# A selective-scan megakernel: the chunk's y is copied first in ACT's step, stores are issued behind their data, and some readers get more links

## The chip, the cores and the metric

The kernel runs on one core of a Trainium2 chip. The metric is the device time of one execution in microseconds; before the change it is 19824.35 us, the median of three runs (19803.24 to 19829.89).

## The reference

Four images of 64 x 64 positions and 96 channels go through four layers. Each layer is `x = x + mixer(norm(x))` and then `x = x + ffn(norm(x))`; the feed-forward part is two small quantised matrix products. The mixer of layer 0 is a gated linear recurrence. The mixers of layers 1 to 3 are selective scans with 192 inner channels, 16 states and four orders of reading the image (by rows, by columns, and both backwards). Cut to what matters:

```
xz = x @ in_proj_w.T;  xi, z = split(xz)
xc = silu(conv3x3_depthwise(xi))
xs = [xc by rows, xc by columns, both reversed]           # 4 orders, L = 4096 steps
dts, B, C = split(xs @ x_proj);  delta = softplus(dts @ dt_proj + bias)
h_t = exp(delta_t * A) * h_(t-1) + delta_t * u_t * B_t    # per channel, 16 states
y_t = sum over states of h_t * C_t  + D * u_t
y = sum of the four orders, put back in place
x = x + (norm(y) * silu(z)) @ out_proj.T
```

## The kernel before

**Stages, chunks and tiles.** After layer 0 (`gated`) the scans of layers 1 to 3 run in 12 stages, one for each image and layer. A stage has two directions, four segments of 1024 steps and three chunks of 128 rows; each chunk has 16 tiles, one for each state. So a stage has 384 tiles and all stages 4608. A tile's *step* in its chunk, 0 to 15, is `n` in the code; `k` counts tiles through all stages.

**What a tile does.** ACT makes the decay `da` (`decays`, line 898), PE spreads a row of B over 128 partitions into `bc` (`b_rows`, 904), DVE multiplies `bc` by `du` and scans (`scan`, 913), ACT copies the last column (`carry`, 929), POOL multiplies `h` by the `c` rows, which SP loads from DRAM two tiles ahead (`c_rows`, 888; `times_c`, 935), and PE adds the product to the chunk's `acc` three tiles later (`accumulate`, 955). When 16 products are in, ACT copies `acc` to `y` and SP stores it (`store`, 966); that falls in step 3 of the next chunk. Buffers: two of `bc`, three of `da` and of `h`, six of `c`, one of `acc`.

**The order on each engine** is the order in which the Python code calls it; no engine reorders. The loop of `scans` (line 993 on) issues for tile `k`: `carry(k-1)`, loads and decay of `k+2`, `b_rows(k+1)`, `times_c(k-1)`, `store` when due, `scan(k)`, and `accumulate(k-3)`. Between the product and the scan of a tile, `beside` (1018) lets other work issue instructions.

**That other work** is written as Python generators, called chains. Every `yield` ends a *link*: what stands between two yields is issued in one go, and the next link at a later turn. The next chunk's preparation and the next segment's get one link per tile. A `Job` (708) does everything between two stages for another image; it gets `rate` links per tile for each of its chains. `between` (616) is such a job: `first` loads the scans' `y` in both orders (3 MB and the first strip), then per strip of 512 positions run `join_orders` (transposes `y_t`, copy to `yt`, statistics), `mixer_out` (normalise, gate, `out_proj`, sum `x1`) and `feed_forward`, then `take_in` (norm, `in_proj`, `z`) and `convolve`. `gate_z` (557) applies silu to `z` and stores it. If a job is not done by tile 356 of a stage, the rest is issued at once.

**SP's queue** issues all transfers, also in order, and waits in front of a transfer whose data or buffer isn't ready.

All operations are recorded by one helper, so the profile shows line 78 for nearly all; they are told apart by the names of their tiles.

Of the kernel before, what the change touches and what calls it, by code (L numbers as in the profile page):

```python
# [21 lines left out]
NS = 16  # L22
# [3 lines left out]
T = 1024  # L26
MM = 512
# [72 lines left out]
def metaformer(ctx: ExitStack, tc: tile.TileContext, x, l0_ab, l0_rest, ssm, ffn, out):  # L100
# [212 lines left out]
    def join_orders(im, s, hold):  # L313

        yr, yc = hold["in"].pop(s)
        if s + 1 < NSTRIP:
            load_y(im, s + 1, hold)
        cols_a, part_c = hold["cols"]
        yt = sb(2, "yt", [128, G, DI])

        def join(ps, g):

            t0, r0 = 128 * g, SR * s + 2 * g
            o, hi = ps[:, g % 2, 0:128], ps[:, g % 2, 128:DI]
            pe.matmul(o, yr[:, t0 : t0 + 128], ident, start=True, stop=False)
            for r in range(2):
                v = cols_a.rearrange("p (c r) -> p r c", r=HW)[:, r0 + r, :]
                pe.matmul(o[64 * r : 64 * r + 64], v, ident, start=False, stop=True)
            yield
            pe.matmul(hi, yc[:, t0 : t0 + 128], ident[0:64, 0:64], start=True, stop=False)  # L330
            for r in range(2):
                for k in range(2):
                    p = slice(64 * k, 64 * k + 64)
                    v = part_c.rearrange("p (c r) -> p r c", r=HW)[p, r0 + r, :]
                    q = 64 * r + 32 * k
                    pe.matmul(
                        hi[q : q + 32], v, ident[p, p], start=False, stop=True, tile_position=(64 * k, q)
                    )

        for pair in range(2):  # L340
            ps = bank("y_t")[:, 0 : 2 * DI].rearrange("p (g c) -> p g c", g=2)
            yield from join(ps, 2 * pair)
            yield
            yield from join(ps, 2 * pair + 1)
            yield
            act.copy(yt[:, 2 * pair : 2 * pair + 2, :], ps)
            release()
            yield pair == 0
        yield
        norm = Norm()  # L350
        yield from norm.measure(yt, DI, 1e-5)
        hold["y", s] = yt, norm

    def mixer_out(im, layer, s, hold):

        w = weights[layer].w
        yt, norm = hold.pop(("y", s))
        zl, zh, xr = load_z(im, s)
        yield from norm.settle()
        yield  # L360
        normalise(yt, yt, DI, norm.r, norm.nm)
        yield
        yield True
        g = []
        for i, (a, b, z) in enumerate(((0, 128, zl), (128, 192, zh))):
            ps = bank("y_c")
            transpose_strip(ps, yt, a, b)
            yield
            v = sb(1, f"u{i}", [128, MM])
            m = b - a  # L370
            sc, bias = (w[0:m, W_LN + 2 * i + k : W_LN + 2 * i + k + 1] for k in range(2))
            act.activation(v[0:m], ps[0:m], AF.Identity, bias=bias, scale=sc)
            release()
            yield i == 0
            g.append(v)
            if i == 0:
                continue
            for v, z, m in ((g[0], zl, 128), (g[1], zh, 64)):
                pool.tensor_tensor(v[0:m], v[0:m], z[0:m], ALU.mult)
                yield  # L380
        yield True
        ps = bank("out_proj")
        for q in range(G):
            t = slice(128 * q, 128 * q + 128)
            o = ps[:, C * q : C * q + C]
            pe.matmul(o, g[0][:, t], w[:, W_OUT : W_OUT + C], start=True, stop=False)
            pe.matmul(o, g[1][0:64, t], w[0:64, W_OUT + C : W_OUT + 2 * C], start=False, stop=True)
            yield
        yield
        x1 = sb(2, "x1", [128, G, C])  # L390
        dve.tensor_tensor(x1, xr, ps[:, 0 : G * C].rearrange("p (g c) -> p g c", g=G), ALU.add)
        release()
        yield
        norm = Norm()
        yield from norm.measure(x1, C, 1e-5)
        hold["x", s] = x1, norm
# [159 lines left out]

    def gate_z(im, s, hold):
        if s < NSTRIP:
            t = slice(s * MM, (s + 1) * MM)
            for z, a in zip(hold["z"].pop(s), (0, 128)):  # L560
                act.activation(z, z, AF.Silu)
                sp.dma_start(out=im.z[a : a + z.shape[0], t], in_=z)

    def convolve(im, layer, s, hold):

        lo, hi = hold["pads"].pop(s)
        taps = weights[layer]
        w = taps.w
        raw = []
        groups = (  # L570
            [(taps.lo[:, t, :], lo[:, t // 3 : t // 3 + SR, t % 3 : t % 3 + HW]) for t in range(9)],
            [(taps.hi[:, t, :], hi[:, 0:SR, t : t + HW]) for t in range(3)]
            + [(taps.hi[0:64, 3 + t, :], hi[0:64, 2 : 2 + SR, t : t + HW]) for t in range(3)],
        )
        for i, group in enumerate(groups):
            ps = bank("conv")
            for at, (lhs, rhs) in enumerate(group):
                pe.matmul(ps, lhs, rhs, start=at == 0, stop=at == len(group) - 1)
                yield
            v = sb(1, f"u{i}", [128, MM])  # L580
            act.copy(v, ps)
            release()
            yield i == 0
            raw.append(v)
        for i, v in enumerate(raw):
            act.activation(v, v, AF.Silu, bias=w[:, W_CB + i : W_CB + i + 1])
        gate_z(im, s + 1, hold)
        yield
        yield
        t = slice(s * MM, (s + 1) * MM)  # L590
        cols_a, part_c = hold["cols"]
        sp.dma_start(out=im.u[0, 0:64, t], in_=raw[0][0:64])
        sp.dma_start(out=im.u[1, 0:64, t], in_=raw[0][64:128])
        sp.dma_start(out=im.u[2, 0:64, t], in_=raw[1][0:64])
        for p, src, dst, c0, nc_ in (
            (slice(0, 128), raw[0], cols_a, 0, HW),
            (slice(0, 64), raw[1], part_c, 0, HW // 2),
            (slice(64, 128), raw[1], part_c, HW // 2, HW // 2),
        ):
            pool.tensor_copy(  # L600
                dst[p].rearrange("p (c r) -> p r c", r=HW)[:, SR * s : SR * s + SR, :],
                src[p].rearrange("p (r c) -> p r c", c=HW)[:, :, c0 : c0 + nc_],
            )
            if p.start or p.stop == 128:
                yield
        if s == NSTRIP - 1:
            yield
            sp.dma_start(out=im.u[1, 64:128, :], in_=cols_a[0:64])
            sp.dma_start(out=im.u[0, 64:128, :], in_=cols_a[64:128])
            for k in range(2):  # L610
                sp.dma_start(
                    out=im.u[2, 64:128, k * L // 2 : (k + 1) * L // 2],
                    in_=part_c[64 * k : 64 * k + 64],
                )

    def between(im, layer, dst=None):
# [8 lines left out]
        def first():  # L625
            if layer:
# [6 lines left out]
                        in_=im.y[2, 64:128, k * L // 2 : (k + 1) * L // 2],  # L633
                    )
                load_y(im, 0, hold)
            yield
            yield
            yield

        yield [Chain(first())]  # L640
        done = {"y": 0, "x": 0, "end": 0}
# [55 lines left out]
        def convolves():  # L697
            yield lambda: done["in"] > 0
            gate_z(im, 0, hold)
            for s in range(NSTRIP):  # L700
                yield lambda: done["in"] > min(s + 1, NSTRIP - 1)
                yield True
# [60 lines left out]
    def prepare_segment(item, sg):  # L763
# [38 lines left out]
        for k in range(2):  # L802
# [3 lines left out]
            yield from project(ps, m, m + NC2, k)  # L806
            act.copy(sg.rows[0:NC2, cols], ps[0:NC2])
            release()
        sp.dma_start(out=sg.cs, in_=sg.rows[0:NC2])

    def prepare_chunk(item):
# [48 lines left out]
    def scans(stages, jobs, pac):  # L860
# [94 lines left out]
        def accumulate(k):  # L955
# [7 lines left out]
                    add_quarters(i, i.yf, stacked, True, False)  # L963
            add_quarters(i, h, stacked, False, n == NS - 1)

        def store(i):
            y = sb(2, "y", [128, T])
            act.copy(y, i.acc)
            for j in range(2):
                for k in range(2):  # L970
                    o = 64 * (j ^ k)
                    t = i.seg * T + k * MM
                    sp.dma_start(
                        out=i.im.y[i.chunk, 64 * j : 64 * j + 64, t : t + MM],
                        in_=y[o : o + 64, j * MM : (j + 1) * MM],
                    )

        chain = segment = None
# [15 lines left out]
        for k in range(last + 5):  # L994
# [23 lines left out]
            def beside():  # L1018
# [5 lines left out]
                        drain(segment, work)  # L1024
                work()

            if 0 <= k - 1 <= last:
                carry(k - 1)
            if k + 2 <= last:
# [5 lines left out]
                b_rows(k + 1)  # L1035
            if 0 <= k - 1 <= last:
                times_c(k - 1)
            if k >= 4 and (k - 4) % NS == NS - 1:
                store(items[(k - 4) // NS])
            if k <= last:  # L1040
                scan(k, beside)
            if 0 <= k - 3 <= last:
                accumulate(k - 3)
            settle()
# [238 lines left out]
    for at in range(len(stages)):  # L1283
        jobs.append([])
        if at + 1 < len(stages):
            im, layer = stages[at + 1]
            jobs[-1].append(Job(between(im, layer - 1), 1.65))

        for im in {10: images[:2], 11: images[2:3]}.get(at, ()):
            jobs[-1].append(Job(between(im, 3, im.dst), 2.6))  # L1290
    with tc.tile_pool(name="pac", bufs=1, space=bass.MemoryType.PSUM) as pac:
        scans(stages, jobs, pac)
    Job(between(images[-1], 3, images[-1].dst), patience=1).finish()
# [123 lines left out]
```

## Time and profile before

| what | us |
|---|---|
| median of three runs | 19824.35 |
| the profiled execution's own time | 19851.56 |
| its span | 19849.8 |
| layer 0, until the first scan | 1962.6 |
| the scans, first start to last end | 17596.9 |
| a stage of layer 1, 2 or 3 (the first ten) | 1428.6 to 1466.9 |
| the last two stages | 1493.6 and 1575.4 |
| after the last scan | 290.2 |
| DVE busy in all | 17714.5 |
| POOL, PE and ACT busy in all | 15487.4, 16411.2 and 12300.6 |

In the profile `h<-da,carry,bc` is the scan, `bc<-du,bc` the product in front of it, `bc<-bs,sel` the spreading on PE, `c<-h,c` POOL's product and `acc<-c,twice` the sum on PE. Behind a bar stands the idle time of the engine just before a group, with what ended it. A wait "DVE bc <- PE bc" means that DVE stood idle in front of the product until PE had written `bc`. The mean granted TensorE clock is 0.814 of full speed.

### The profile page before, as it was taken

The numbers are of one execution on the slowest core, as the hardware profiler recorded it, in microseconds if no ns is written. First come the engines' busy times: TensorE is split into PE (matmuls) and PEld (weight loads), VectorE is DVE, ScalarE is ACT, GpSimd is POOL, SyncE is SP. The second block draws the span as 40 slices with busy tenths as digits, with TensorE's granted clock in tenths as the row PEclk, the third lists the DMA queues.
The fourth block names the chain that finished last, engine by engine and source line by source line (L and its number), as shares of the span: only waits on it lengthen the run. The fifth ranks groups of instructions, "written<-read, shape, count | busy, mean of one in ns | idle before, by whom it ended". The sixth has DMA issues, their size and how long they took to land. (4 is left out here: it accounts for less than half of the span.)

```text
span 19849.8 us, 224201 instructions
## 1 busy us (share of the span) xinstructions
PE 16411.2 (83%) x70656; PEld 4815.3 (24%) x70656; DVE 17714.5 (89%) x13832; ACT 12300.6 (62%) x19398; POOL 15487.4 (78%) x10086
## 2 busy tenths in 40 slices
PE   8898788787787888888887887887888888888786
PEld 3333121121121222222222222222222222222223
DVE  6656999999999999999999999999999999989884
ACT  3444665665665665665665665666666666666664
POOL 3333888888888888888888888888888888888884
PEclk9899786796787787887797797797797787888886
DMA  0001666666666666666666666666666666666663
GB/s 19 15 22 36 164 179 176 166 182 173 168 185 174 168 180 184 167 183 180 167 182 177 170 183 181 167 183 182 165 188 174 174 185 173 170 188 169 165 176 91
DMA packets 1233005, 3142.45 MB, mean 158 GB/s; under 512 B 428048, under 2 KB 428176, under 8 KB 1225680
## 3 DMA queue, kind: packets, MB, share of 16 engines
q1 hardware_dynamic: 1231824, 3128.11, 59.1%
q8 instruction: 570, 9.34, 0.2%
q14 instruction: 611, 5.01, 0.1%
HBM read 2819.03 MB, written 308.28 MB: 158 GB/s over the span
## 5 line engine op out<-in xcount | busy, mean ns | idle before, releaser
L78 POOL TENSOR_TENSOR c<-h,c 128x1024 f32<-128x1024 f32 (+1 forms) x4992 | 11327.0, 2275 | 3532.4 <-DVE h L78 1479.8
L78 DVE TENSOR_TENSOR_SCAN h<-da,carry,bc 128x1024 f32<-128x1024 f32 x4608 | 10797.2, 2343 | 532.1 <-POOL c L78 17.0
L78 PE MATMUL acc<-c,twice 64*64 64x512 f32 x36864 | 6212.0, 750 | 21.8 <-POOL c L78 21.7
L78 ACT ACTIVATE da<-delta,decay 128x1024 f32<-128x1024 f32 x4608 | 5280.5, 1147 | 1497.1 <-DVE h L78 1474.3
L78 DVE TENSOR_TENSOR bc<-du,bc 128x1024 f32<-128x1024 f32 x4608 | 5567.8, 1208 | 499.7 <-PE bc L78 473.6
L78 PE MATMUL bc<-bs,sel 96*128 96x512 bf16 x9216 | 3392.6, 456 | 2350.8 <-DVE h L78 2239.7
L78 ACT COPY carry<-h 128x1 f32<-128x1 f32 x3456 | 649.7, 188 | 3366.3 <-DVE h L78 3360.1
L78 PEld LDWEIGHTS <-sel 96*128 96x128 bf16 x9216 | 551.3, 101 | 7304.2 <-DVE h L78 5491.0
L78 PEld LDWEIGHTS acc<-c,twice 64*64 64x64 f32 x36864 | 1132.6, 153 | 2805.1 <-issue 1888.6
L78 ACT ACT_TABLE_LOAD x1158 | 1485.7, 1283 | 37.8 <-DVE mv L78 21.5
L78 PE MATMUL conv<-pad,tap_lo 128*128 128x512 f32 x1728 | 904.9, 633 | 0.0
L78 PE MATMUL dt_proj<-rows,w 12*128 12x512 f32 x1152 | 832.1, 809 | 6.1 <-ACT delta L78 6.1
L78 ACT ACTIVATE du<-e,ones 128x1024 f32<-128x1024 f32 x576 | 659.3, 1145 | 200.8 <-POOL delta L78 195.7
L78 ACT ACTIVATE c<-c,l_bias 128x512 f32<-128x512 f32 x384 | 263.4, 686 | 771.8 <-PE c L78 770.4
L78 POOL TENSOR_TENSOR delta<-delta,du 128x1024 f32<-128x1024 f32 x288 | 679.4, 2359 | 71.4 <-ACT du L78 69.3
L78 PE MATMUL x_proj_b<-u,xp 128*108 128x512 f32 x1152 | 694.4, 720 | 42.5 <-DMA xp<-in_ssm 14.5
L78 PE MATMUL x_proj_c<-u,xp 128*32 128x512 f32 x1152 | 632.0, 662 | 76.0 <-ACT rows L78 67.1
L78 POOL TENSOR_TENSOR e<-e,du 128x1024 f32<-128x1024 f32 x288 | 679.1, 2358 | 2.4 <-ACT du L78 2.4
L78 POOL TENSOR_TENSOR du<-delta,u 128x1024 f32<-128x1024 f32 x288 | 679.6, 2360 | 0.1
L78 POOL TENSOR_TENSOR delta<-delta,e 128x1024 f32<-128x1024 f32 x288 | 678.1, 2355 | 0.1
L78 PE MATMUL conv<-pad,tap_hi 128*128 128x512 f32 (+1 forms) x1152 | 597.5, 620 | 0.6 <-ACT u L78 0.4
L78 DVE TENSOR_TENSOR_SCAN h<-da,l_carry,bc 128x512 f32<-128x512 f32 x384 | 491.5, 1280 | 42.1 <-POOL c L78 2.0
(154 smaller groups left out, 15512.1 us busy)
## 6 DMA issues: line engine op xcount, KB each, us to landing
c<-cs SPq DMA_DIRECT2D x9216, 256.0 KB, 4.1
u<-u SPq DMA_DIRECT2D x288, 512.0 KB, 6.6
y<-y SPq DMA_DIRECT2D x1152, 128.0 KB, 3.2
y<-y SPq DMA_DIRECT2D x144, 512.0 KB, 6.9
xr<-x SPq DMA_DIRECT2D x224, 192.0 KB, 5.3
u<-u SPq DMA_DIRECT2D x288, 128.0 KB, 3.5
pad<-y SPq DMA_DIRECT2D x288, 128.0 KB, 4.9
z<-zl SPq DMA_DIRECT2D x96, 256.0 KB, 2.0
```

The source lines that it names most:

```text
L78: ins = f(*a, **k).ins
```

## The change

- `join_orders` and `mixer_out` get one more `yield` each: one ahead of the statistics of `yt`, one ahead of the sum `x1` on DVE.
- `gate_z` applies silu alone; the stores of `z` are in a new `store_z`, two links later.
- `first` waits nine links instead of three after its loads, where the layer is 1 or more.
- `prepare_segment` gets one more `yield` ahead of the store of `cs`.
- `store` is cut in two: `take` copies `acc` to `y` as the first of ACT's instructions in the tile, ahead of `carry`; the transfers of `store` are issued behind `scan` and what `beside` issues.
- The jobs' rates go from 1.65 to 1.72 and from 2.6 to 2.8 (layer 0's job keeps 2.6).

```diff
@@ join_orders
             yield pair == 0
+        yield
         yield
         norm = Norm()
         yield from norm.measure(yt, DI, 1e-5)
@@ mixer_out
             yield
         yield
+        yield
         x1 = sb(2, "x1", [128, G, C])
@@ gate_z
     def gate_z(im, s, hold):
         if s < NSTRIP:
+            for z in hold["z"][s]:
+                act.activation(z, z, AF.Silu)
+
+    def store_z(im, s, hold):
+        if s < NSTRIP:
             t = slice(s * MM, (s + 1) * MM)
             for z, a in zip(hold["z"].pop(s), (0, 128)):
-                act.activation(z, z, AF.Silu)
                 sp.dma_start(out=im.z[a : a + z.shape[0], t], in_=z)
@@ convolve
         gate_z(im, s + 1, hold)
         yield
         yield
+        store_z(im, s + 1, hold)
@@ between, first
-            yield
-            yield
-            yield
+            for _ in range(9 if layer else 3):
+                yield
@@ between, convolves
             gate_z(im, 0, hold)
+            yield
+            yield
+            store_z(im, 0, hold)
@@ prepare_segment
             release()
+        yield
         sp.dma_start(out=sg.cs, in_=sg.rows[0:NC2])
@@ scans
+        def take(i):
+            i.y = sb(2, "y", [128, T])
+            act.copy(i.y, i.acc)
+
         def store(i):
-            y = sb(2, "y", [128, T])
-            act.copy(y, i.acc)
...
-                        in_=y[o : o + 64, j * MM : (j + 1) * MM],
+                        in_=i.y[o : o + 64, j * MM : (j + 1) * MM],
@@ scans, the loop
+            full = items[(k - 4) // NS] if k >= 4 and (k - 4) % NS == NS - 1 else None
+            if full is not None:
+                take(full)
             if 0 <= k - 1 <= last:
                 carry(k - 1)
...
                 times_c(k - 1)
-            if k >= 4 and (k - 4) % NS == NS - 1:
-                store(items[(k - 4) // NS])
             if k <= last:
                 scan(k, beside)
+            if full is not None:
+                store(full)
@@ the jobs
-            jobs[-1].append(Job(between(im, layer - 1), 1.65))
+            jobs[-1].append(Job(between(im, layer - 1), 1.72))
...
-            jobs[-1].append(Job(between(im, 3, im.dst), 2.6))
+            jobs[-1].append(Job(between(im, 3, im.dst), 2.8))
```

## The prediction

> **What bounds the kernel now.** I read the page first, then the waits of DVE, PE and POOL between 1986 and 19560 us (the scans), then the timeline around the longest idle stretches.
>
> ```profile
> span 19849.8 us, 224201 instructions
> ...
> PE 16411.2 (83%) x70656; PEld 4815.3 (24%) x70656; DVE 17714.5 (89%) x13832; ACT 12300.6 (62%) x19398; POOL 15487.4 (78%) x10086
> ...
> L78 DVE TENSOR_TENSOR_SCAN h<-da,carry,bc 128x1024 f32<-128x1024 f32 x4608 | 10797.2, 2343 | 532.1 <-POOL c L78 17.0
> ...
> L78 DVE TENSOR_TENSOR bc<-du,bc 128x1024 f32<-128x1024 f32 x4608 | 5567.8, 1208 | 499.7 <-PE bc L78 473.6
> ```
>
> DVE paces the scans. One tile costs a product of 1.21 us, a scan of 2.34 and about 0.1 between them: the undisturbed tile of the timeline is 3.6 us. The scans run from 1963 to 19560, 17597 us, in which DVE is busy 17115; another 0.5 ms is the short step between product and scan. Idle stretches over 0.3 us add up to only 627 us, 23 of which are the very first tile. So no edit here can win more than about 600 us (3%), and what it wins is a DVE wait that goes.
>
> ```profile
> DVE bc L78 <- PE bc L78: 473.6, 295, 22.2
> DVE rows L78 <- ACT bs L78: 29.6, 15, 3.9
> DVE x L78 <- PE out_proj L78: 29.3, 24, 2.9
> DVE st L78 <- ACT yt L78: 22.0, 22, 2.7
> ```
>
> Those are DVE's waits in the scans: total, count, longest. Nearly all are for `bc`, which PE writes. PE works in order, so a late `bc` means that PE was held in front of it. By step of the chunk (16 tiles), the idle before `bc` is largest in steps 4 and 5 (61 and 86 us), just behind the copy of `y`, then 9 (76), 0 (54, with the first tile's 23) and 6 (44, where the jobs' first loads are read).
>
> ```profile
> PE acc L78 <- ACT y L78: 156.9, 146, 2.9
> ...
> PE y_t L78 <- DMA pad<-y: 94.3, 11, 24.4
> ```
>
> These are two of PE's own waits in the same stretch; both are what the change goes for.
>
> **Part 1: nine links instead of three behind the first loads.** A job reads 3 MB (`cols_a`, `part_c`) and the first strip before its first `y_t`. The trace shows 11 such reads in the scans: eight at a stage's start (DVE idle 4.9 to 6.1 us each, 43.3 in all) and three later (22.2, 14.3 and 11.2), each of these followed by one more wait of 2.57: 99 us. The built orders put the first `y_t` in tile 7 of a stage instead of 4, and 5 tiles behind the late loads instead of 2: three tiles, 10.8 us, more. PE's own wait at a stage's start, 3.8 to 6.8 us, would be gone. But does DVE get all of it?
>
> ```profile
> 6264.07 2.35 POOL L78 TENSOR_TENSOR c<-h,c 128x1024 f32<-128x1024 f32 x1 [1.25 <-DVE h L78]
> ...
> 6272.41 2.35 DVE L78 TENSOR_TENSOR_SCAN h<-da,carry,bc 128x1024 f32<-128x1024 f32 x1
> ...
> 6275.27 0.77 PE L78 MATMUL y_t<-ident,pad 128*128 128x128 f32 x2 [6.62 <-DMA pad<-y]
> ...
> 6277.49 4.71 POOL L78 TENSOR_TENSOR c<-h,c 128x1024 f32<-128x1024 f32 x2 [11.06 <-DMA c<-cs]
> ...
> 6280.63 1.23 DVE L78 TENSOR_TENSOR bc<-du,bc 128x1024 f32<-128x1024 f32 x1 [5.88 <-PE bc L78]
> ...
> 6281.99 2.35 DVE L78 TENSOR_TENSOR_SCAN h<-da,carry,bc 128x1024 f32<-128x1024 f32 x1
> ```
>
> No. POOL is idle for 11.06 us at the same place, and for another reason: its `c` rows were issued behind the 3 MB and landed 17 us later (6259.2 to 6276.3), where the median is 4.1. More links do not move those. `h` has three buffers, so the scan at 6281.99 needs POOL's product of three tiles before, the first of the pair from 6277.49, which ended at 6279.84. Without PE's wait that scan would be due at 6272.41 + 3.6 = 6276.0 and start at about 6279.9: of 5.9 us some 3.9 stay and 2 go. Eight times 2 is 16 us. The same working for the late three (next scans due every 3.6 us, held by the product three tiles before) leaves 14.0 of 24.8, 3.0 of 13.8 and 6.1 of 16.9: 32 us. Together 48; the ends are 25 (what is left is worse) and 99.
>
> The Trainium skill says the same of the queue, and it speaks against this edit: by "DMA: Bandwidth & Descriptors", section "Queues, rings and completion order", each DMA engine takes descriptors in ring order, and all of SP's transfers share one row. By that rule alone the `c` rows must wait for the 3 MB whatever the reader does, which gives the 48; if it did not hold, the 99.
>
> **Part 2: y's copy first in ACT's step.** The copy stood behind `carry` and the decay two tiles ahead, which wait for the scan. `acc` has one buffer, so PE's first matmul of the next chunk waits for the copy, and `bc` waits behind it.
>
> ```profile
> 15909.79 0.61 ACT L78 ACTIVATE zh<-zh 64x512 f32<-64x512 f32 x1
> 15910.31 0.17 ACT L78 COPY carry<-h 128x1 f32<-128x1 f32 x1
> 15910.49 1.28 ACT L78 ACT_TABLE_LOAD   x1
> 15911.78 1.15 ACT L78 ACTIVATE da<-delta,decay 128x1024 f32<-128x1024 f32 x1
> 15912.84 0.99 ACT L78 COPY y<-acc 128x1024 f32<-128x1024 f32 x1
> ```
>
> Here `acc` was complete at 15905.5 and the copy could have started when `zh` ended, 2.4 us sooner; DVE idled 3.35 us before the `bc` behind it. I took all 288 copies so: start minus the later of "`acc` complete" and "ACT free of what stands ahead of `carry`". The mean is 0.8 us, the largest about 3.4. Where a wait for `bc` over 0.3 us follows within four tiles, the smaller of the two is won: 37 places, 43 us, those of part 1 left out. At all 37 POOL's product of three tiles before leaves over 5 us, so it holds nothing. What the copy can now hold up when `acc` is late: `carry` (read 48 tiles later), the decay (1.15 us) and the job's ACT work. `acc` ends at the median 0.75 us after the scan, at the 95th percentile 5.1; then the decay ends at 5.1 + 1.0 + 0.2 + 1.15 = 7.5, and its scan starts at 8.5 at the earliest. On these numbers it costs nothing; were the cover gone, up to 1.3 us in a third of the 288 chunks, 125 us. I keep 43, with ends of 20 and 60.
>
> **Part 3: one more link before two DVE readers.** In the built order 80 of 96 strips have the statistics of `yt` one tile behind ACT's copy; after the change 11 have, the others two. Of 22.0 us about 19 go. The sum of `out_proj` hardly moves (72 at one tile become 64): 3 of 29.
>
> **Part 4: transfers issued behind their data.** The stores of `z`, `cs` and `y` move on SP's queue, so that the `c` rows queued behind them are not held. In the scans POOL waits 329.3 us for `c` rows (92 times), but 129 of them belong to part 1, and of the rest only some 23 us of DVE idling follow within five tiles. I take 3, ends 0 and 23. In the stage before the scans (1963 us; strips of 54.5 us without the job, 60 to 72 with it) and in the tail (290 us, whose first `y_t` waits 22.7 us for loads with nothing left to put in front) I take 0, ends -10 and +10 each.
>
> **Part 5: everything else moves.** With the longer chains and 1.72 links per tile (1.65), strips meet other steps of the chunk. The jobs end at tile 330 of a stage (333), well before the forced end at 356, so no burst comes. PE's work per tile is the same in sum. Priced by the strips of before: `out_proj` issued in step 11 is followed within three tiles by 1.65 us of DVE idling on the mean, step 14 by 0.99, step 7 by 2.94; 9, 17 and 8 strips stand there, and 27, 25 and 8 will. All steps so weighted go from 85 to 113 us. POOL adds `delta` in step 11, and the gating products that `out_proj` needs queue there. Transposes give +19 (`ff_xt`), -7 (`in_xt`) and +2 (`y_c`), partly for the same tiles. I take 25 us lost; ends 75 lost and 40 won. ACT's table loads go from 1158 to 1103; 55 of 1.28 us are 71 us, on an engine at 62%: 0 on the path.
>
> **Sum.** 48 + 43 + 19 + 3 + 3 - 25 = 91 us won. The profiled execution took 19851.6 us (span 19849.8), 27 above the median of 19824.35; from it the sum gives 19760.6, and from the median 19733.
>
> **Rivals.** *The new places eat it:* of the 116 us won, 75 or more are lost in part 5. For it: 27 strips in step 11. Against: the same load per tile. Time 19785 to 19860, likeliest 19800. *Slower:* one mechanism, `out_proj` held by POOL. If the strips in steps 11 and 14 cost what the worst rows show (PE's longest wait for the product is 4.1 us, DVE then idles 3.6 to 5.0), 52 strips lose 3 us each where 26 lost 32 in all: 124 us. With the 19 of `ff_xt`, and against the low ends of parts 1 and 2 (45) and the 25 of parts 3 and 4, that is some 73 slower, 19897. It is even at 1.6 us per strip and 40 slower at 2.3. Against it: the 17 strips in step 14 cost 0.99 now. *More than forecast:* `c` rows land sooner or the new places are free: 99 + 60 + 22 and 20 from part 5 are 201, 19623. *It does not do what it says:* the built order excludes that; the copy stands ahead of `carry` in every chunk.
>
> **How the numbers follow.** Forecast (gain 40 to 170) 0.66; more 0.06; eaten, within 40 us, 0.13; slower 0.15. A measurement here can tell about 0.2%, 40 us. Faster takes the first two and a little of the third, which reaches its edge: 0.71, no change 0.13, slower 0.16. The range takes in the forecast's low side and most of the eaten case: 19650 to 19830.
>
> **What would show it.** Right: `y_t` from `pad<-y` leaves PE's waits or falls under 15 us, `acc` from ACT `y` falls from 156.9 under 70, `st` from `yt` to about 3, DVE's wait for `bc` to about 360, while POOL's idling for `c` rows at a stage's start stays at 10 us and DVE's `h` from POOL `c` grows from 17 to about 50. Wrong: `bc` from PE stays at 470 or rises, with PE's `out_proj` from POOL `u` well above 63.4.

## The result, and the profile after

The changed kernel takes 19942.12 us (median of 5 runs, 19933.14 to 19963.6) against 19829.89 for the kernel before beside it (5 runs). The ratio is 1.0057, with a 95% interval of 1.0044 to 1.0070: 0.57% of the time before are 113 us lost, where 91 won were forecast. These are the lines of its page that answer to those shown of before:

```profile
span 19944.0 us, 224196 instructions
...
L78 DVE TENSOR_TENSOR_SCAN h<-da,carry,bc 128x1024 f32<-128x1024 f32 x4608 | 10795.5, 2343 | 572.9 <-POOL c L78 57.7
...
L78 DVE TENSOR_TENSOR bc<-du,bc 128x1024 f32<-128x1024 f32 x4608 | 5567.9, 1208 | 573.0 <-PE bc L78 546.6
...
L78 ACT COPY y<-acc 128x1024 f32<-128x1024 f32 x288 | 291.1, 1011 | 768.9 <-PE acc L78 758.0
```

DVE's two great groups take as long as before, and DVE as a whole is busy 5 us longer (17719.9), so nearly all of the loss is idle time. The wait in front of the product has grown from 473.6 to 546.6 us, the scan's wait for POOL's `c` from 17.0 to 57.7. The last line is new among the costly waits: ACT now stands 758.0 us in front of `y`'s copy, against this line of before:

```profile
L78 ACT COPY y<-acc 128x1024 f32<-128x1024 f32 x288 | 288.3, 1001 | 185.8 <-PE acc L78 185.3
```

DVE's waits in the scans, 1986 to 19650 us (total, count, longest):

```profile
DVE bc L78 <- PE bc L78: 546.6, 376, 6.3
DVE h L78 <- POOL c L78: 57.7, 17, 11.9
...
DVE st L78 <- ACT yt L78: 5.6, 9, 1.7
```

The longest wait for `bc` has gone from 22.2 to 6.3 us, and yet their number has gone from 295 to 376 and their sum up. PE's waits in the same stretch say which old holds went and which came:

```profile
PE x_proj_c L78 <- ACT rows L78: 112.5, 54, 3.0
PE out_proj L78 <- POOL u L78: 80.8, 50, 5.0
...
PE acc L78 <- ACT y L78: 52.9, 91, 2.2
...
PE x_proj_b L78 <- ACT yt L78: 41.7, 26, 3.6
...
PE y_t L78 <- DMA pad<-y: 19.8, 3, 11.5
```

`acc` from ACT `y` fell from 156.9 to 52.9 and `y_t` from `pad<-y` from 94.3 to 19.8, as the change intends. In their place stand `x_proj_c` waiting for ACT's copy to `rows` and `x_proj_b` waiting for ACT's copy to `yt`. Of the latter the kernel before has no such wait; of the former it has this:

```profile
PE x_proj_c L78 <- ACT rows L78: 67.1, 53, 3.0
```

So there are two questions: is it the copy's move, or is it the strips' new places?

### The profile page after: what moved, and what is told of

It reads as the page before. It is cut to its first block, busy times and chain, and to the rows that moved or that the text cites. A ratio compares the mean times of both kernels' runs of the same rounds, so it can differ in the third digit from the quotient of the medians.

```text
span 19944.0 us, 224196 instructions
## 1 busy us (share of the span) xinstructions
PE 16563.0 (83%) x70656; PEld 4824.2 (24%) x70656; DVE 17719.9 (89%) x13832; ACT 12199.7 (61%) x19343; POOL 15496.3 (78%) x10086
## 5 line engine op out<-in xcount | busy, mean ns | idle before, releaser
L78 DVE TENSOR_TENSOR_SCAN h<-da,carry,bc 128x1024 f32<-128x1024 f32 x4608 | 10795.5, 2343 | 572.9 <-POOL c L78 57.7
L78 PE MATMUL acc<-c,twice 64*64 64x512 f32 x36864 | 6300.4, 761 | 40.0 <-POOL c L78 39.9
L78 DVE TENSOR_TENSOR bc<-du,bc 128x1024 f32<-128x1024 f32 x4608 | 5567.9, 1208 | 573.0 <-PE bc L78 546.6
L78 ACT ACT_TABLE_LOAD x1103 | 1415.1, 1283 | 37.5 <-DVE mv L78 21.3
L78 PE MATMUL x_proj_b<-u,xp 128*108 128x512 f32 x1152 | 738.9, 761 | 87.3 <-ACT yt L78 41.7
L78 ACT COPY y<-acc 128x1024 f32<-128x1024 f32 x288 | 291.1, 1011 | 768.9 <-PE acc L78 758.0
```

Of the source, the lines that this page charges most:

```text
L78: ins = f(*a, **k).ins
```

## The experiments

All were timed in five rounds beside the kernel before; ratios are to that, with 95% intervals, and differences in us are the ratio's share of its median (19838.75 to 19848.06 in the four series). Two theories stand against each other in the first expectations: P, that the parts win what was priced and the strips' new places lose more; and A (later H), that the copy waits at the head of ACT's queue with ready work behind it.

**One part at a time.** The first four kernels are the one before with one part each.

```diff
 # e1_take
+            if full is not None:
+                take(full)            # y's copy, ahead of carry and the decay
             if 0 <= k - 1 <= last:
                 carry(k - 1)
...
                 scan(k, beside)
+            if full is not None:
+                store(full)           # y's transfers
```


> The kernel before with one part of the change alone: y's copy first in ACT's step, y's transfers behind the scan. No link moves, so every strip stays at its step of the chunk. Theory P (the parts win what was priced, and the new places of the strips lose more): 43 us faster, ratio 0.9978, PE's wait for ACT y down from 157 to about 50 us, DVE's wait for bc down by about 40. Rival A (the copy at the head of ACT's step holds up ACT's other work, which frees banks for PE): no faster or slower, ratio 1.000 to 1.005, with new PE waits for ACT rows, yt or pad. Rival N (what the copy wins is given back in the next steps): ratio 1.000.

Measured: 19939.81 us, ratio 1.0047 (1.0034 to 1.0059), 93 us slower.

```diff
 # e2_first: three yields -> nine
+            for _ in range(9 if layer else 3):
+                yield
```


> The kernel before with nine links behind the first loads alone. Theory P: the wait for the loads gives back 48 us, but all strips of a job's first half stand 3 to 4 tiles later, so that the time lies between 50 us faster and 100 us slower, and PE's waits for other things than pad change by more than 50 us. Rival A (the copy is the cause): 48 us faster, ratio 0.9976, since the copy is untouched. DVE h from POOL c grows from 17 to about 55 us in both.

Measured: 19797.5 us, ratio 0.9977 (0.9969 to 0.9986), 46 us faster.

```diff
 # e3_links: join_orders and mixer_out
         yield
+        yield
         norm = Norm()
...
         yield
+        yield
         x1 = sb(2, "x1", [128, G, C])
```


> The kernel before with the two additional links in front of DVE's readers alone. Theory P: 22 us won at the readers (yt, out_proj) and an unknown sum lost or won in the strips' new places, 100 us either way. Rival A: 22 us faster, ratio 0.9989.

Measured: 19811.93 us, ratio 0.9979 (0.9971 to 0.9988), 42 us faster.

```diff
 # e4_rates
-            jobs[-1].append(Job(between(im, layer - 1), 1.65))
+            jobs[-1].append(Job(between(im, layer - 1), 1.72))
...
-            jobs[-1].append(Job(between(im, 3, im.dst), 2.6))
+            jobs[-1].append(Job(between(im, 3, im.dst), 2.8))
```


> The kernel before with the rates 1.72 and 2.8 alone. Nothing waits less or more by itself. Theory P: the time moves by several tens of us, likely slower (20 to 120 us), since strips meet other steps of the chunk. Rival A: ratio 1.000 within 0.1%.

Measured: 19810.71 us, ratio 0.9982 (0.9973 to 0.9991), 36 us faster.

So the copy's move, priced at 43 won, costs 93, as A has it, and each other part wins alone. For e4 both expectations missed: P had it likely slower, A had it unchanged. And the 124 us that the other three win alone are not in the changed kernel, which is as slow as e1 (1.0057 and 1.0047, with overlapping intervals): something is still to be found.

**Which half of the move costs: ACT's order or SP's?**

```diff
 # e5_copy: the copy first, y's transfers where they were
+            if full is not None:
+                take(full)
             if 0 <= k - 1 <= last:
                 carry(k - 1)
...
-                store(items[(k - 4) // NS])
+                store(full)
             if k <= last:
                 scan(k, beside)
```


> The kernel before, with y's copy first in ACT's step and y's transfers issued where they were (so SP's order is that of before). Theory H (the copy at the head of ACT's queue waits for PE's acc with ready work behind it, the decay and the copies that free PE's banks): nearly all of the 92 us that the whole move cost, 60 to 92 slower (ratio 1.003 to 1.0047), with ACT's y from PE acc near 715 us in 243 waits, PE's x_proj_c from ACT rows near 120 us, and PE's acc from ACT y near 40. Rival Q (the loss comes from y's transfers, which now stand behind others in SP's queue): the 43 us of part 2 are won, ratio 0.998, and x_proj_c from ACT rows stays near 67.

Measured: 19904.26 us, ratio 1.0034 (1.0021 to 1.0046), 67 us slower. ACT waits 719.6 us in front of the copy, `acc` waits for `y` only 33.2. Two lines of its waits, in the scans:

```profile
DVE bc L78 <- PE bc L78: 497.6, 294, 22.8
...
PE x_proj_c L78 <- ACT rows L78: 126.6, 63, 4.4
```

The profiled execution is 54 us longer than that of before, 24 of which are in this wait for `bc` (473.6 before); the rest is spread over DVE's smaller waits.

```diff
 # e6_transfers: the copy where it was, y's transfers behind the scan
-                store(items[(k - 4) // NS])
+                take(full)
             if k <= last:
                 scan(k, beside)
+            if full is not None:
+                store(full)
```


> The kernel before, with ACT's order unchanged and only y's transfers issued behind the scan and the work beside it. Theory H: ACT loses nothing, and what SP's order costs is small: 0 to 25 us slower (ratio 1.000 to 1.0013), with PE's x_proj_b from DMA u near 30 us (almost none before). Rival Q: most of the 92 us, ratio 1.004 or more.

Measured: 19857.61 us, ratio 1.0011 (1.0002 to 1.0019), 22 us slower; `x_proj_b` now waits 21.3 us (1.6 before) for the loads `u<-u`, which stand behind `y`'s stores on SP's queue. 67 and 22 make up nearly the 93 of the whole move, each within some 25 us: about three quarters are ACT's order.

The timeline shows how. These are lines of the kernel before, around the copy in the first stage's third chunk (start, duration, engine, operation; in brackets the idle time ahead):

```profile
2092.35 1.14 ACT L78 ACTIVATE da<-delta,decay 128x1024 f32<-128x1024 f32 x1
...
2097.00 1.01 ACT L78 COPY y<-acc 128x1024 f32<-128x1024 f32 x1 [3.51 <-PE acc L78]
...
2103.81 0.56 ACT L78 COPY rows<-x_proj_c 32x512 f32<-32x512 f32 x1
...
2104.42 1.90 PE L78 MATMUL x_proj_c<-u,xp 128*32 128x512 f32 x4 [1.80 <-ACT rows L78]
```

And the same place in e5_copy:

```profile
2096.72 1.01 ACT L78 COPY y<-acc 128x1024 f32<-128x1024 f32 x1 [7.10 <-PE acc L78]
...
2097.72 1.15 ACT L78 ACTIVATE da<-delta,decay 128x1024 f32<-128x1024 f32 x1
...
2104.66 0.56 ACT L78 COPY rows<-x_proj_c 32x512 f32<-32x512 f32 x1
...
2105.27 2.44 PE L78 MATMUL x_proj_c<-u,xp 128*32 128x512 f32 x4 [2.93 <-ACT rows L78]
...
2110.68 1.23 DVE L78 TENSOR_TENSOR bc<-du,bc 128x1024 f32<-128x1024 f32 x1 [2.55 <-PE bc L78]
```

Before, ACT made the decay while `acc` was being completed, and waited 3.51 us. In e5 it waits 7.10 with the decay ready behind the copy, and does it afterwards. ACT is then 1.13 us back (`rows` is 0.85 us later, in a run that stood 0.28 us ahead here). The decay itself is in time: its scan is two tiles away. But in the same tiles ACT has a softplus, a table load and the copy to `rows` to do, and PE's next `x_proj_c` needs what `rows` reads out. PE waits 2.93 us instead of 1.80, and the spreading of `bc` queues behind it: DVE idles 2.55 us where it did not idle.

ACT's 1.13 us are the smaller part of that. From the start of `x_proj_c` to that of `bc` PE takes 4.77 us in e5 for the same instructions that took 3.17 before. The granted clock is 0.50 in e5 from 2106.6 to 2109.8, behind PE's wait, and 1.00 before from 2096.6 to 2120.0; the eight `acc` matmuls of that stretch take 1.92 us instead of 1.09. This is this place alone: over all scans the mean clock of both runs is 0.81.

**Which instruction pays.**

```diff
 # e15_mid: carry, copy, decay; y's transfers where they were
             if 0 <= k - 1 <= last:
                 carry(k - 1)
+            if full is not None:
+                take(full)
             if k + 2 <= last:
```


> The kernel before, with y's copy between carry and the decay and y's transfers where they were. Theory H says that the decay (1.15 us, with its table load) behind a copy that waits is what falls back, not carry (0.2 us): as slow as with the copy in front of both, 40 to 75 us slower (1.002 to 1.0038). Rival (carry, or the place at the very head of the step, is what matters): within 20 us of before (0.999 to 1.001).

Measured: 19887.01 us, ratio 1.0027 (1.0016 to 1.0037), 54 us slower, `x_proj_c` from `rows` 122.6. So the decay behind the copy is enough, as H has it; the intervals of e5 and e15 overlap, so what `carry` adds is not settled. DVE's wait for `bc` grew only to 477.1 us in its profiled execution, which was its fastest (19877.16), so the way from ACT to DVE is shown by e5's rows and not by this run's.

**The rest of the change without the copy's move.**

```diff
 # e7_after_no_take: the changed kernel, but
-                take(full)
...
-                store(full)
...
+                store(items[(k - 4) // NS])   # copy and transfers, as before
```


> The changed kernel, with y's copy and y's transfers back at their old places; the other five edits stay. Theory H: the other parts add up as they did one by one (50, 36 and 37 us), 60 to 125 us faster than the kernel before (ratio 0.9937 to 0.997). Rival (the edits that shift the strips eat each other's gain): 0.998 to 1.001.

Measured: 19895.36 us, ratio 1.0029 (1.0018 to 1.0039), 58 us *slower*. Both expectations missed: three parts that win 46, 42 and 36 us alone lose together.

> The kernel before, with z's stores two links later and one more yield ahead of the store of cs, nothing else. Part 4 priced this at 3 us won with ends of 0 and 23 (ratio 0.9988 to 1.000). Rival: the added links shift the strips to other tiles and the time goes 20 us or more up (ratio 1.001 or more).

(e8_behind: `z`'s stores two links later and the yield ahead of `cs`' store, on the kernel before.) Measured: 19842.71 us, ratio 1.0001 (0.9993 to 1.001): nothing, as part 4 had it for these two.

What meets what was then read out of the built orders: a tile has a *meeting* if PE has `out_proj` in it and also `y_t`, `ff_y` or `x_proj_b`. The next four runs go by it (theory M: meetings are what costs).

```diff
 # e9_oldrates: e7_after_no_take with 1.65 and 2.6
 # e10_links_rates: e3_links and e4_rates together
 # e11_first_rates: e2_first and e4_rates together
 # e12_twelve: e7_after_no_take, but
-            for _ in range(9 if layer else 3):
+            for _ in range(12 if layer else 3):
```


> The changed kernel with y's copy and transfers at their old places and the jobs' rates back at 1.65 and 2.6: the nine links, the two added links and the stores behind their data stay. Theory M (what costs time is strips that meet each other and the next segment's work in one tile: out_proj stands in the same tile as x_proj_b 41 times and as ff_y 47 times with all five edits, but 9 and 28 times here, 21 and 38 in the kernel before): 50 to 110 us faster than before (ratio 0.9945 to 0.9975). Rival (any two edits that lengthen the chains spoil each other, whatever meets): 0.999 to 1.003.

Measured: 19851.27 us, ratio 1.0007 (0.9998 to 1.0015). A miss for M, and as its rival had it: the nine links and the two links, which win 46 and 42 us alone, win nothing together.

> The kernel before, with the two added links and the rates 1.72 and 2.8, without the nine links and the rest. Theory M (out_proj meets x_proj_b 44 times and ff_y 44 times): the two edits, which won 36 and 37 us alone, together win nothing or lose, 0 to 80 us slower (1.000 to 1.004), with PE's out_proj from POOL u near 80 us and x_proj_b from ACT yt near 40. Rival (the nine links are what goes badly with the others): 40 to 80 us faster, 0.996 to 0.998.

Measured: 19947.69 us, ratio 1.0053 (1.0040 to 1.0067), 105 us slower. The links and the rates are the worst pair, by more than M had said.

> The kernel before, with the nine links and the rates 1.72 and 2.8, without the two added links and the rest. Theory M (out_proj meets x_proj_b 19 times and ff_y 19 times): 50 to 100 us faster (0.995 to 0.9975), with x_proj_b from ACT yt under 5 us. Rival (longer first waits and higher rates spoil each other): 0.999 to 1.003.

Measured: 19789.09 us, ratio 0.9972 (0.9962 to 0.9981), 56 us faster, as M had it: the lowest ratio of all, though its interval overlaps with those of e2, e3, e4 and e12. The pair without the two links is the one that keeps most of its gains.

> The changed kernel with y's copy and transfers at their old places, and twelve links behind the first loads instead of nine: three links more, which only move all strips by two tiles against the chunks. Theory M (out_proj meets x_proj_b 20 times and ff_y 37 times, as in the kernel before; with nine 41 and 47): the loss goes, 30 to 100 us faster than the kernel before (0.995 to 0.9985). Rival (the added links and the rate cost by themselves): as with nine links, 1.002 to 1.004.

Measured: 19794.32 us, ratio 0.9977 (0.9968 to 0.9986), 46 us faster. The text on record is wrong in one point: the three links move the strips not by two tiles each but by one to 15 (`out_proj` in tiles 62 and 63 of a stage goes to 61 and 62, that in 75 to 77 goes to 90 and 91).

Three empty links are thus worth 103 us (1.0029 to 0.9977), with the same work in all. I added up DVE's idle stretches over 0.3 us by the tile of the stage they stand in front of, over the fourth to eleventh stage. The same tiles come back in each of these eight stages: 46 to 48, 64 to 66 and 78 hold 105 us in the changed kernel, 107 in e7, 97 in e10, 18 in the kernel before and none in e12. This is tile 64 in the changed kernel:

```profile
7972.02 2.38 POOL L78 TENSOR_TENSOR c<-h,c 128x1024 f32<-128x1024 f32 x1
...
7974.33 2.37 POOL L78 TENSOR_TENSOR du<-delta,u 128x1024 f32<-128x1024 f32 x1
...
7976.63 1.29 POOL L78 TENSOR_TENSOR u<-u,zh 64x512 f32<-64x512 f32 x1
...
7977.97 0.74 PE L78 MATMUL out_proj<-w,u 64*128 64x96 f32 x2 [3.80 <-POOL u L78]
7978.42 6.97 POOL L78 TENSOR_TENSOR c<-h,c 128x1024 f32<-128x1024 f32 x3
...
7978.64 0.66 PE L78 MATMUL ff_y<-w,hq 128*128 128x96 fp8e5 x6
...
7979.10 1.38 PE L78 MATMUL out_proj<-w,u 128*128 128x96 f32 x4
...
7980.41 1.98 PE L78 MATMUL acc<-c,twice 64*64 64x512 f32 x8
...
7983.47 1.23 DVE L78 TENSOR_TENSOR bc<-du,bc 128x1024 f32<-128x1024 f32 x1 [3.56 <-PE bc L78]
...
7989.28 1.23 DVE L78 TENSOR_TENSOR bc<-du,bc 128x1024 f32<-128x1024 f32 x1 [2.10 <-PE bc L78]
```

At the turn of a chunk POOL makes the next chunk's `du`, 2.37 us on top of its product. The strip's second gating product `u` stands behind both, `out_proj` waits 3.80 us for it, `ff_y` of another strip and four more `out_proj` are queued behind, then 8 matmuls of `acc`, and only then `bc`: DVE idles 3.56 and 2.10 us, in each of the eight stages. In e12_twelve the strip is there a tile earlier:

```profile
7919.93 1.27 POOL L78 TENSOR_TENSOR u<-u,zh 64x512 f32<-64x512 f32 x1
...
7921.26 0.46 PE L78 MATMUL out_proj<-w,u 64*128 64x96 f32 x2 [0.53 <-POOL u L78]
...
7925.79 2.37 POOL L78 TENSOR_TENSOR du<-delta,u 128x1024 f32<-128x1024 f32 x1
```

`u` is made ahead of `du`, and PE waits 0.53 us.

The wait behind `du` is not new, though: in the kernel before, `out_proj` waits for `u` in tile 63 of all eight stages (3.65 us at 15285.07, 3.3 on the mean), and DVE idles 1.24 us behind it. What is new is the work behind the wait: from the start of the late `out_proj` to that of `bc` PE takes 4.36 us in the changed kernel and 2.58 before, where neither `ff_y` nor more of `out_proj` stands between.

**Do the two halves add up, and does the count foretell?**

```diff
 # e13_after_twelve: the changed kernel, copy's move and all, but
-            for _ in range(9 if layer else 3):
+            for _ in range(12 if layer else 3):
 # e14_rate170: e7_after_no_take with 1.70 instead of 1.72
```


> The changed kernel with twelve links behind the first loads instead of nine, nothing else. If the strips' meetings (worth 103 us between nine and twelve links without the copy's move) and the copy's move (55 to 92 us) are the two whole causes and add up: 0 to 45 us slower than the kernel before (ratio 1.000 to 1.0023), 65 to 110 faster than the changed kernel, with PE's x_proj_c from ACT rows still near 115 us and DVE's bc from PE bc near 440. Rival (the copy's move brings the meetings' loss back, or is itself the larger part): 1.003 or more. Rival (the copy's move costs only where strips meet): 0.998 or less.

Measured: 19872.48 us, ratio 1.0014 (1.0005 to 1.0023), 28 us slower than before and some 85 faster than the changed kernel. `x_proj_c` waits 128.1 us for `rows`, DVE's `bc` 427.9, both near what was said: the halves add up, within the intervals.

> The changed kernel with y's copy and transfers at their old places and the jobs' rate at 1.70 instead of 1.72 (the last jobs' stays 2.8). In the built order of a middle stage out_proj then meets x_proj_b, ff_y or y_t in one tile in 3 tiles instead of 11 (6 with twelve links, 6 in the kernel before). Theory M: at least as fast as with twelve links, 40 to 110 us faster than before (0.9945 to 0.998). Rival (the meetings are not what costs; the added links and a rate near 1.72 are): 1.001 to 1.003.

Measured: 19857.22 us, ratio 1.0008 (0.9999 to 1.0017). A miss: the tiles 46 to 48, 64 to 66 and 78 cost nothing here, but others do (74 with 4.1 us and 121 with 3.6 on the mean of the same eight stages; 121 costs 2.6 in e12 too), and the scan's wait for POOL's `c` is 84.5 us. M's counter does not forecast; that a strip's place decides is shown, which place is good is not.

## Why the prediction was wrong

**Part 1 held.** 48 won were priced, 46 measured alone (e2). That the size is so near is in part luck: e2 moves the strips as well, and DVE's wait for `bc` fell by 135.5 us there, more than the 99 of the late loads. Of the signs, `y_t` from `pad<-y` fell to 19.8, where under 15 was said, and DVE's scans wait 57.7 us for POOL's `c`, where about 50 were said. The `c` rows do stay late: POOL idles for them for 10.5 to 12.1 us at the start of each of the fourth to eleventh stages.

**Part 2 failed, at the sentence "On these numbers it costs nothing".** The wait that it was to remove did go: `acc` from ACT `y` fell under 70 as said. The cost was looked for on one path alone, from the decay to its scan, and that path is indeed clean: `h` waits for `da` 7.5 us in all (4.9 before). The same sum named a size, "up to 1.3 us in a third of the 288 chunks", 125 us, and set it to nothing; that was meant for the decay's own scan, so that it comes near what was lost is luck. What bears the cost is ACT's other work: ACT's copies out of PE's results come later (`x_proj_c` waits 126.6 us for `rows` in e5, 67.1 before), PE waits for them in order, and `bc` stands behind. The whole move costs 93 us on the kernel before and 55 on top of the other parts (113 less 58), so the term of 43 won, with nothing set for `y`'s transfers, was 98 to 136 off; 67 of the 93 are ACT's order.

**Part 3 held, part 4 in part.** `st` from `yt` fell to 5.6 us (3 said), and e3 won 42 where 22 were priced; the rest is put down to places, which this run does not show by itself. In part 4 the stores of `z` and `cs` moved nothing (e8), as priced; `y`'s transfers, which it took for nothing or a gain, cost some 22 us on the kernel before (e6): it looked at the `c` rows behind the stores and not at the loads `u<-u`.

**Part 5 was mis-sized.** 25 lost were taken, with ends of 75 lost and 40 won. Alone, a mere change of rates even won 36 us (e4). The other parts were priced at 73 won and measured together (e7) at 58 lost: what is left for the places is 131, outside the end of 75. The step at fault is the weighing "by the strips of before", by step of the chunk alone. In the stalls that were read, what counts is not the step but what else stands there: POOL's `du` at the turn of the chunk and a second strip's `ff_y` in tile 64, `y_t` in front of tile 47, a segment's `x_proj_b` in front of tile 78. Those repeat in each stage, so one bad tile is paid eight times. The two errors, 98 and 106 us, make up the 204 between 91 won and 113 lost; as both are taken from e7, they must.

**One reading was wrong without consequence.** DVE is busy for 16468 us in the scans and not 17115; the 627 us of idling, which bound the gain, are right.

**The rivals.** The slower one named `out_proj` held by POOL, with DVE idling 3.6 to 5.0 us; tile 64 is near that, but in step 0 behind `du`, not in steps 11 and 14, the wait itself was there before, and PE's total for it grew only from 63.4 to 80.8. That set of tiles is one of three, 53 us with the kernel before at 17. "The new places eat it" was the right family for part 5, with too small a price. The sign that was named for being wrong, `bc` staying or rising, came; the sign that went with it, `out_proj` from `u` "well above 63.4", hardly did.

## What to carry to other kernels

An instruction that waits, moved to the front of an in-order queue, delays everything ready behind it; follow each of those to its readers on every engine, not only the one that the old order was made for. Here a copy moved ahead of 1.3 us of ready work cost more than the wait it removed. And where background work shares an engine with a periodic loop, a change of its phase is a change of its own: gains of single edits that each shift the phase do not add up, so measure the combination, and try some phases of it before judging an edit.

## What the runs showed of the hardware that was not expected

The granted clock differed among kernels that do the same work: 0.804 in e10 (span 19938.6), 0.806 in the changed kernel, 0.814 before and 0.819 in e3 (19790.0). It goes roughly with the time, but e5 at 19903.9 us shows 0.814 and e11 at 19804.2 shows 0.813. These are means: the clock rows of the traces hold only 1.00 and 0.50, and at 0.50 the eight `acc` matmuls of a tile take 1.98 us instead of 1.09 and the two of `bc` 1.04 instead of 0.60. The median `bc` matmul is 0.39 us in all runs and hides this.

The kernel before shows what that is worth at one place. Over the two tiles up to tile 65 PE has the same work in each of the fourth to eleventh stages. In six of them the mean clock there is 0.77 to 0.80, and the two tiles take 8.7 to 9.0 us; in the ninth and the eleventh it is 0.50, and has been for two or three tiles, and they take 12.5, with 3.6 us more of DVE idling. In the changed kernel tile 64 stands at 0.50 as well (7971.1 to 7994.9). So the clock sets part of what a bad place costs; how much of the 103 us between e7 and e12 goes that way no run separates.

ACT had 55 table loads fewer (1158 to 1103, 1.28 us each) and was 101 us less busy, in a kernel that got slower: nothing of that reached the end.
